# A table of priorities redrawn: the static order of a Restormer block on five engines

## The chip, the cores and the metric

The kernel runs on one core of a Trainium2 chip. The metric is the device time of one execution in microseconds (us); lower is better. All arithmetic is in float32.

## What is computed

The input x has 16 images of 128 channels and 96 x 96 pixels. One block is applied to it: a layer norm over channels, an attention whose matrix is channels by channels (8 heads of 16 channels) and which needs a sum over all pixels of an image, a residual, a second layer norm, and a feed-forward part (128 to 512 channels, a depthwise 3 x 3 convolution, a gelu, 512 back to 128 channels) with a residual.

```python
x_hwc = x.transpose(0, 2, 3, 1)
xn1 = _layernorm(x_hwc, ln1_w, ln1_b)
x = x + _attention(xn1, wq, wk, wv, wp).transpose(0, 3, 1, 2)   # softmax(l2norm(q) l2norm(k)^T) v, per head
xn2 = _layernorm(x.transpose(0, 2, 3, 1), ln2_w, ln2_b).transpose(0, 3, 1, 2)
h1 = jnp.einsum('bchw,oc->bohw', xn2, w_in[:, :, 0, 0])
h2 = lax.conv_general_dilated(h1, w_dw, ..., feature_group_count=HID)
x = x + jnp.einsum('bchw,oc->bohw', gelu(h2), w_out[:, :, 0, 0])
```

## The kernel before

**Tiling.** Channels lie on the 128 partitions. An image is cut into 8 bands of 12 rows (1152 pixels), a band into 3 units of 4 rows (384 pixels). With 16 images there are 128 bands. The 512 hidden channels are 4 chunks of 128. A job is one chunk of one band in the depthwise convolution (conv_job, L1143); in some bands the fourth chunk is done by PE instead (by_matmuls, L1259). There are 467 jobs that use the vector engines.

**Work by engine.** These are the kinds of operations, under the names that the table uses:

- PE (TensorE): forth_a, forth_b (transposes for the statistics, L868), gram (L916), back_a, back_b (transposes back, L964), mix (the attention's matrix on x, L818), hidden (128 to 512 channels, L1162), conv (nine taps by matmuls, L1274 and L1280), out (512 to 128, L1315).
- DVE (VectorE): stats_a, stats_b (L876), place_b (normalized x into the ring, L968), residual (L824), tap (multiply and add one shifted tap: L1190 for the first and the last of a job, L1194 between them), add (the last residual, L1322).
- ACT (ScalarE): copied_a, copied_b (L905, L973), place_a (L970), mixed (L827), halo (L1158), kept (the hidden chunk out of a PSUM bank, L1167), products (one tap times its weight, L1178), gelu (L1211), conv_gelu (L1292).
- POOL (GpSimd): variance_a, variance_b (L881), power_a, power_b (L885), scaled_a (L909), merge (adds a product and the unshifted chunk into the one buffer merged, L1181; a second addition at L1184), and it issues the adding transfers add_x (L830), add_last (L1203) and add_first (L1206).
- SP (SyncE) issues load_a (L795) and store (L1326).

The letters a and b stand for the first and second normalization.

**What sets the order.** The program is written out in a fixed order of instructions for every engine. Before that, a planner in the kernel (class Plan, L228) simulates the engines with a duration for each operation. An operation is ready when what it depends on is done and its buffers are free. Of the ready operations of an engine, the one with the lowest place goes first (order, L274; dispatch, L313). The resulting order is then emitted (the last lines of tile_restormer_block), and on the chip every engine takes its own instructions strictly in that order and waits for semaphores.

A place counts in jobs: an operation of job 100 has a base near 100. To it comes a number by kind, and a shift by kind and stretch, where a stretch is 15 places:

```python
def place_at(kind, place, i=1):
    of = kind if i else kind + "_0"
    return Place(place + (AT[of] + SHIFTS.get(max(0, int(place // STRETCH)), {}).get(of, 0)), RANK.get(kind, 0))
```

AT (L51) has a number for each kind, from some -3600 to some +4600. Against these, the 467 places of the whole run are few, so the sum of AT and shift mostly says which kind goes first within a stretch, and the place itself decides among operations of one kind. SHIFTS (L66) has 32 rows, one for each stretch of 15 places, and up to 53 entries in a row. Place (L219) adds RANK to the priority alone, and leaves it out of the turn in which buffers of some pools are given (IN_TURN, L50).

**Shared things.** The kinds compete for four PSUM banks (h), one accumulator of three banks (acc), the one buffer merged, 8 product buffers (pr), 8 gelu buffers (h3), 4 transposed buffers (zT), 5 and 2 bands of x (xb, x1).

Of the kernel before, what the change touches and what calls it, by code (L numbers as in the profile page):

```python
# [66 lines left out]
    0: dict(load_w=1.9, zeros=-8.4, load_a=-22.8, forth_a=-1.1, stats_a=-0.3, variance_a=-0.3, power_a=-8.1,  # L67
        merge=-300.7, gram=0.2, back_a=-0.2, place_a=-1660.1, attention=-276.4, mix=-21.7, residual=-23.2,
        mixed=530.5, forth_b=40.5, stats_b=-118.7, variance_b=14.1, power_b=605.1, back_b=0.1, place_b=1.6,
        halo=4.3, kept=986.6, products=-7.1, add_last=329.8, tap=-1.6, add_first=1.7, gelu=7.1, conv=-6,  # L70
        conv_gelu=0.4, out=0.2, add=-660.9, store=1.7, mix_0=-899, residual_0=-622, gram_0=0.9, forth_a_0=18.5,
        stats_a_0=-2.4, stats_b_0=19.6, scaled_a_0=-65.5, copied_a=-60.9, back_a_0=-6.5, back_b_0=0.2,
        place_a_0=399.7, place_b_0=1296.2, late=10.6, load_a_0=4.4, load_dw=229.6, units=8.6, variance_a_0=619.5,
        power_a_0=-469.8, variance_b_0=-341, power_b_0=-17.1),
    1: dict(load_a=-14.5, forth_a=0.1, stats_a=14.8, variance_a=1354, power_a=1176.9, merge=637, scaled_a=46.3,
        gram=-0.1, back_a=0.1, place_a=1.6, attention=-12.1, mix=-4.5, mixed=403.6, add_x=1946.3, forth_b=-6.6,
        stats_b=-1.9, variance_b=-52.3, power_b=5.8, back_b=170.3, place_b=-0.2, halo=-1066.6, hidden=-3.3,
        kept=923, products=1, add_last=-6.7, tap=0.7, add_first=1488, gelu=1.5, conv=0.7, conv_gelu=0.9, out=-0.4,
        add=2.8, copied_a=379.4),
    2: dict(forth_a=0.2, stats_a=-3.5, variance_a=-8.2, merge=0.8, scaled_a=-9.6, gram=3281.1, place_a=1229.9,  # L80
        mixed=38.9, forth_b=-125.8, stats_b=576.6, variance_b=-252.3, power_b=-0.5, back_b=-1367.9, place_b=-21.3,
        halo=-1033.7, kept=0.2, add_last=1838.5, add_first=19.2, gelu=-95.7, conv=-0.2, conv_gelu=0.1, add=-688.1,
        store=-2.9, copied_b=-10.5),
    3: dict(load_a=0.3, stats_a=-421.1, variance_a=1.7, power_a=1940.7, merge=360.1, scaled_a=19.9, gram=-3.7,
        back_a=-1.6, place_a=-1386.7, mix=-3.2, mixed=-1368.8, add_x=331.4, forth_b=9.5, stats_b=-631.1,
        power_b=84.1, place_b=-406.8, halo=-5.4, kept=976.7, products=0.3, add_last=0.8, tap=0.1, add_first=1358.3,
        gelu=2.1, conv=-2.9, conv_gelu=-0.3, add=-1929.6, store=-1489.9, copied_a=4.3),
    4: dict(load_a=-0.5, forth_a=0.4, stats_a=-0.7, power_a=24.6, merge=-2.2, scaled_a=1377.6, back_a=-152.2,
        place_a=-15.7, mixed=-9.8, add_x=2.6, forth_b=73.3, stats_b=12.2, variance_b=-15.1, power_b=-8.5,
        back_b=0.1, place_b=2076.2, halo=5, kept=185.5, products=-0.1, add_last=6.5, tap=0.5, add_first=-10.8,  # L90
        gelu=-13.4, conv=-3.1, conv_gelu=0.7, out=0.1, add=-664.4, store=1113.3, copied_a=-1138.6),
    5: dict(load_a=0.1, stats_a=-1.1, variance_a=-313.3, power_a=1.2, merge=-12.5, scaled_a=1035.8, gram=-3.2,
        back_a=-3.1, place_a=-265.5, attention=-0.6, mix=2.8, mixed=137.1, add_x=-6.9, forth_b=-29.6,
        stats_b=-638.6, variance_b=771.6, power_b=45, back_b=-404.6, place_b=146, halo=-0.5, kept=200.1,
        add_last=2.7, add_first=-1.7, gelu=-2, conv=0.4, conv_gelu=0.3, add=2.9, store=1134, copied_a=1.4,
        copied_b=18.3),
    6: dict(forth_a=-0.2, stats_a=15.7, variance_a=-46.9, power_a=976.2, scaled_a=-8.2, gram=2277.6, back_a=-2,
        place_a=-7.5, mix=0.1, mixed=-346.5, add_x=-1.2, forth_b=3.4, stats_b=0.2, variance_b=0.1, power_b=37.6,
        back_b=-0.5, place_b=1358.9, halo=49.9, kept=-465.7, products=-0.1, gelu=21, conv=-22.3, conv_gelu=0.1,
        add=-599.3, store=3342.4, copied_a=-381.6),  # L100
    7: dict(forth_a=0.2, stats_a=-1.6, variance_a=1309.9, power_a=2424.9, merge=0.2, scaled_a=4976.2, gram=-27.8,
        back_a=11.1, place_a=176.5, attention=-0.4, mix=0.7, mixed=-5.3, add_x=358.3, forth_b=7.9, stats_b=1.4,
        variance_b=-1.7, power_b=8.5, back_b=0.6, place_b=19.7, halo=1.9, kept=864.1, products=-1, add_last=342.7,
        tap=-0.6, add_first=15.3, gelu=5, conv=3346, conv_gelu=-0.5, store=1090.3, copied_a=-967.2,
        copied_b=1704.6),
    8: dict(load_a=-2.4, forth_a=1.3, stats_a=0.3, variance_a=-4.2, power_a=-4.3, merge=7.7, scaled_a=670.4,
        gram=2291.6, place_a=24.6, mix=-0.3, mixed=1600.2, add_x=-36.8, forth_b=57.3, stats_b=1042.9,
        variance_b=-17, power_b=-0.3, back_b=-0.2, place_b=2469.7, halo=-2888.4, kept=1099.2, add_last=-33.7,
        tap=0.8, gelu=-6.8, conv=-6.2, conv_gelu=0.9, out=0.1, add=-406.4, copied_a=2.7),
    9: dict(load_a=-1.9, stats_a=-0.2, variance_a=-0.1, power_a=23.8, merge=-25, scaled_a=11.3, gram=-7.9,  # L110
        back_a=-0.3, place_a=-511.8, attention=-1.8, mix=-2.4, mixed=-1119.9, add_x=320.8, forth_b=-16.7,
        stats_b=-566.6, variance_b=8.9, power_b=10.1, back_b=-0.2, place_b=-0.8, kept=-0.8, products=-0.3,
        add_last=-16.7, tap=0.3, add_first=6.8, gelu=19.2, conv=-5.3, conv_gelu=0.1, add=0.7, store=-980.3,
        copied_a=25.1),
# [5 lines left out]
    11: dict(forth_a=-0.7, stats_a=13.2, variance_a=367, power_a=5322.9, merge=-21.3, scaled_a=1837.4, gram=3416.9,  # L120
        back_a=-339.2, attention=-1, mix=-1.1, mixed=640.8, add_x=2.6, forth_b=4.6, stats_b=10.1, variance_b=-16.9,
        power_b=4.6, back_b=-0.2, place_b=565.6, halo=13.3, hidden=-0.7, kept=859.2, add_last=23.5, tap=0.7,
        add_first=-6.9, conv=1.5, conv_gelu=-0.2, add=1024.5, store=4493.9),
    12: dict(load_a=10.3, forth_a=5.5, stats_a=9.9, variance_a=-0.8, merge=-188.3, gram=0.1, place_a=-1371.9,
        mix=-1.2, mixed=-1155.8, add_x=-847.4, forth_b=-21.3, stats_b=581.5, variance_b=21.3, power_b=-52.5,
        place_b=1.1, halo=-3.3, kept=17.6, products=0.4, tap=1, add_first=9.7, gelu=14.3, conv=-0.1, out=-0.4,
        add=959.9, store=-103.4, copied_a=-1417.6),
    13: dict(load_a=-1, forth_a=-1.5, stats_a=0.3, variance_a=157, power_a=-144.7, merge=1628.9, scaled_a=23.4,
        gram=14.4, back_a=10.4, place_a=973.7, attention=-0.4, mix=-3.2, mixed=-508.1, add_x=16.4, forth_b=3.7,
        stats_b=-1506.7, variance_b=1583.4, power_b=1787.5, place_b=-0.3, halo=-2.1, kept=1321.3, products=0.7,  # L130
        add_last=-985.5, add_first=57.2, gelu=-1.1, conv=-0.4, conv_gelu=0.2, add=12.2, store=4, copied_a=0.3,
        copied_b=42),
    14: dict(load_a=9.9, forth_a=-0.7, stats_a=1.9, variance_a=920.6, power_a=-677.5, merge=14.3, gram=-1.7,
        place_a=-1663.1, mix=1.4, mixed=-558.3, add_x=52.8, forth_b=-30.6, stats_b=-645, variance_b=7.6,
        power_b=-18.6, back_b=-448.9, place_b=637.9, halo=35.3, products=-0.1, add_last=25.3, tap=-0.2,
        add_first=2.1, gelu=-10.5, conv=-0.7, conv_gelu=0.9, add=8.7, copied_a=375),
    15: dict(load_a=-1.6, variance_a=-6.2, power_a=708.9, merge=-556.4, scaled_a=2876.1, gram=0.5, back_a=68.5,
        place_a=-266, attention=-1, mix=1.8, mixed=-3.4, forth_b=11.3, variance_b=553.6, power_b=11.4, back_b=-0.7,
        halo=16.8, kept=870.2, add_last=6.4, gelu=-15.6, conv=-1.7, add=4.5, store=-113.3, copied_a=1.1,
        copied_b=-10.1),  # L140
# [12 lines left out]
        copied_b=4622.1),  # L153
# [1246 lines left out]
```

## Time and profile before

| what | value |
|---|---|
| median of 3 runs | 3971.78 us (3965.01 to 3973.48) |
| the profiled execution | 3976.05 us |
| its span, first to last instruction | 3974.3 us |
| mean granted TensorE clock | 0.998 |
| HBM read and written | 148.85 MB and 75.50 MB |
| moved by all DMA queues | 777.42 MB |

The profiled execution is 4.27 us longer than the median of the runs, and its span leaves 1.75 us for what lies around it. Most of the moved bytes are transfers from on-chip memory to on-chip memory that add: add_last and add_first, 466 of each with 576 KB.

A line of a group reads: code line, engine, operation, output and inputs by the program's names, shape, count, then busy us and mean ns of one, then the engine's idle time before such instructions and what ended it. PEld is the loading of weights that belongs to a matmul. A float32 matmul here is two instructions of each kind, a transpose one. A line of waits reads: who waited for whom, us in total, times, longest us.

### The profile page before, as it was taken

How to read it: one execution, taken by the hardware profiler on the slowest of the kernel's cores; microseconds unless marked ns; L12 is line 12 of the kernel's file. 1: busy time of each engine (PE TensorE's matmuls, PEld its weight loads, DVE VectorE, ACT ScalarE, POOL GpSimd, SP SyncE). 2: the span in 40 equal slices, each digit the busy share in tenths (PEclk: the TensorE clock that was granted, in tenths of full speed). 3: DMA queues.
4: the chain of work that ended last, by engine and by line, in shares of the span. 5: the costliest groups of instructions: out<-in, count | busy, mean ns of one | idle time of the engine just before them, and what ended most of it. 6: DMA issues, size and time to landing. Idle time of an engine off the chain costs nothing.

```text
span 3974.3 us, 50973 instructions
## 1 busy us (share of the span) xinstructions
PE 3892.4 (98%) x16760; PEld 2521.7 (63%) x16760; DVE 3834.8 (96%) x4390; ACT 3558.1 (90%) x5186; POOL 3379.4 (85%) x3107
## 2 busy tenths in 40 slices
PE   8999999999999999999999999999999999999999
PEld 7566666666666666666666666666666666665555
DVE  7999999999999999999999999999999999999998
ACT  3989989989999999999989989999899999998886
POOL 5998988898898988988888888888888888888674
PEclk9999999999999999999999999999999999999999
DMA  3999999999999999999999999999999999999996
GB/s 100 187 191 204 200 200 198 199 202 198 210 201 209 203 198 203 200 210 201 194 202 197 207 201 194 205 197 206 189 192 206 203 207 201 203 197 183 191 189 146
DMA packets 191691, 777.42 MB, mean 196 GB/s; under 512 B 22208, under 2 KB 23616, under 8 KB 191424
## 3 DMA queue, kind: packets, MB, share of 16 engines
q0 software_dynamic: 151920, 622.33, 82.6%
q1 hardware_dynamic: 38784, 151.75, 10.2%
q8 instruction: 132, 2.16, 0.2%
q14 instruction: 135, 1.11, 0.1%
q10 hardware_dynamic: 720, 0.07, 0.0%
HBM read 148.85 MB, written 75.50 MB: 56 GB/s over the span
## 4 chain that ended last, share of the span: by engine, by line
PE 58%; DVE 14%; ACT 10%; DMA 7%; POOL 6%; issue 5%; POOLq 0%; DVEq 0%; ACTq 0%
PE h L1315 15%; PE h L1162 14%; PE h L1274 13%; DVE acc L1194 6%; DMA h<-pr 5%; ACT pr L1178 5%; PE h L818 4%; PE h L964 4%; PE g L916 3%; PE h L868 3%; DVE acc L1190 3%; DVE h L1190 2%; ACT h L1167 2%; POOL merged L1181 2%; DMA pr<-pr 2%
## 5 line engine op out<-in xcount | busy, mean ns | idle before, releaser
L1178 ACT ACTIVATE pr<-h,ratio 128x1152 f32<-128x1152 f32 x1494 | 1837.2, 1271 | 37.6 <-DMA h<-pr 12.6
L1194 DVE SCALAR_TENSOR_TENSOR acc<-h,ratio,acc 128x1152 f32<-128x1152 f32 (+1 forms) x1308 | 1810.3, 1384 | 7.7
L1181 POOL TENSOR_TENSOR merged<-pr,h 128x1152 f32<-128x1152 f32 x466 | 1238.1, 2657 | 100.5 <-DVE acc L1190 54.7
L1162 PE MATMUL h<-xn,winT 128*128 128x384 f32 (+2 forms) x2802 | 1088.0, 496 | 16.0 <-ACT h L1167 9.2
L1315 PE MATMUL h<-h,woutT 128*128 128x384 f32 x3072 | 1086.2, 488 | 1.7 <-ACT h L1167 1.1
L1274 PE MATMUL h<-xn,comp 128*128 128x380 f32 (+2 forms) x2430 | 895.0, 482 | 2.2 <-ACT h L1167 1.5
L1167 ACT COPY h<-h 128x384 f32<-128x384 f32 (+2 forms) x1401 | 652.9, 493 | 192.4 <-PE h L1162 187.5
L1315 PEld LDWEIGHTS h<-h,woutT 128*128 128x128 f32 x3072 | 565.2, 190 | 359.3 <-ACT h L1167 7.8
L1162 PEld LDWEIGHTS h<-xn,winT 128*128 128x128 f32 x2802 | 500.0, 190 | 326.6 <-issue 34.2
L1190 DVE SCALAR_TENSOR_TENSOR acc<-h,ratio,merged 128x1152 f32<-128x1152 f32 x466 | 686.6, 1473 | 20.9 <-POOL merged L1184 10.1
L1206 POOL DMA_DIRECT2D h<-pr x466 | 463.3, 994 | 241.9 <-DVE h L1190 57.5
L1190 DVE SCALAR_TENSOR_TENSOR h<-h,ratio,acc 128x1152 f32<-128x1152 f32 x467 | 655.2, 1403 | 3.4
L1211 ACT ACTIVATE h<-h,ksum 128x1152 f32<-128x1152 f32 (+2 forms) x586 | 616.0, 1081 | 46.4 <-DMA h<-pr 45.6
L1274 PEld LDWEIGHTS h<-xn,comp 128*128 128x128 f32 x2430 | 430.6, 189 | 235.2 <-issue 17.1
L1203 POOL DMA_DIRECT2D pr<-pr x466 | 478.7, 1040 | 103.1 <-ACT pr L1178 73.4
L885 POOL TENSOR_TENSOR ve_b<-ve_b,mhalf 128x4 f32<-128x4 f32 x288 | 366.0, 1277 | 7.9
L909 POOL TENSOR_TENSOR zT<-zT,ve_a 128x512 f32<-128x512 f32 x270 | 331.3, 1232 | 8.6
L885 POOL TENSOR_TENSOR ve_a<-ve_a,mhalf 128x4 f32<-128x4 f32 x288 | 318.6, 1109 | 15.3
L868 PE MATMUL h<-ident,x 128*128 128x128 f32 x2244 | 317.0, 275 | 13.7 <-ACT xn L970 4.9
L868 PEld LDWEIGHTS h<-ident,x 128*128 128x128 f32 x2244 | 263.6, 142 | 96.4 <-issue 38.6
L818 PE MATMUL h<-xn,mwT 128*128 128x384 f32 x768 | 289.1, 490 | 7.7 <-ACT h L1167 3.2
L916 PEld LDWEIGHTS g<-zT 128*128 128x128 f32 x2160 | 269.9, 191 | 40.2 <-POOL zT L909 11.0
(190 smaller groups left out, 3967.0 us busy)
## 6 DMA issues: line engine op xcount, KB each, us to landing
pr<-pr POOLq DMA_DIRECT2D x466, 576.0 KB, 7.8
h<-pr POOLq DMA_DIRECT2D x466, 576.0 KB, 7.7
x<-in_x_dram SPq DMA_DIRECT2D x128, 576.0 KB, 7.5
out_dram<-x SPq DMA_DIRECT2D x127, 576.0 KB, 4.6
x<-in_x_dram POOLq DMA_DIRECT2D x123, 576.0 KB, 9.1
out_dram<-x SPq DMA_DIRECT2D x3, 192.0 KB, 1.9
h<-in_L_conv_w_in_dram SPq DMA_DIRECT2D x1, 256.0 KB, 3.4
h<-in_L_conv_w_out_dram SPq DMA_DIRECT2D x1, 256.0 KB, 3.6
```

The lines of the kernel that those rows point to most:

```text
L868: nc.tensor.transpose(d["pT", q][:, k, :], xt[:, j * P : (j + 1) * P], ident)
L885: nc.gpsimd.tensor_tensor(rstd, rstd, mhalf, ALU.pow)
L1162: nc.tensor.matmul(rows(ph), lhsT=winT[:, n, :], rhs=window(xn, r0 + r, e - r, 1), start=True, stop=True)
L1167: nc.scalar.copy(window(h1_, r, e - r, 1), rows(d.pop(("ph", r))))
L1178: nc.scalar.activation(to, shifted(t), AF.Copy, scale=ratio[:, n, t : t + 1])
L1181: nc.gpsimd.tensor_tensor(merged, d["pr", dma_taps[0]], shifted(UNIT), ALU.add)
L1190: nc.vector.scalar_tensor_tensor(to, shifted(t), ratio[:, n, t : t + 1], also, ALU.mult, ALU.add)
L1194: nc.vector.scalar_tensor_tensor(to, shifted(t)[:, lo:hi, cut], ratio[:, n, t : t + 1], to, ALU.mult, ALU.add)
L1203: nc.gpsimd.dma_start(out=d["pr", dma_taps[1]], in_=d["pr", t], accum_op=ALU.add)
L1211: nc.scalar.activation(h3, h3, AF.Gelu, bias=ksum[:, z, n : n + 1])
L1274: nc.tensor.matmul(d["pc"][:, lo:hi, cut], lhsT=comp[:, t, :], rhs=window(xn, r0 + dy, UR, dx)[:, lo:hi, cut], start=(t == order[0]), stop ...
L1315: nc.tensor.matmul(rows(d["po"]), lhsT=woutT[:, n, :], rhs=h3s[g, n][:, s * UR : (s + 1) * UR, :], start=(k == 0), stop=(k == NCH - 1),)
```

## The change

Only the table SHIFTS is new. It was searched once more, from the former table, with three other sets of scattered durations. AT, RANK, STRETCH, the planner with its durations, and all operations stay. The former table has 882 entries, the new one 917. Over both, 21 entries are equal, 162 differ by under 1, 186 by 1 to 10, 235 by 10 to 100 and 410 by 100 or more; all 32 stretches are touched. As one example, this is the stretch of places 150 to 164:

```diff
@@ -64,141 +64,142 @@
 STRETCH = 15
 SHIFTS = {
...
-    10: dict(forth_a=-0.1, stats_a=-18.6, variance_a=213.9, power_a=-1.6, merge=-0.3, scaled_a=1679, gram=3360.3,
-        back_a=-0.8, place_a=-13.6, mix=-3.6, mixed=503.8, add_x=829.5, forth_b=1.4, stats_b=16.4,
-        variance_b=1422.9, power_b=15, back_b=0.5, place_b=1532, halo=9, hidden=1.3, kept=1393.5, products=0.1,
-        add_last=-363.1, add_first=-14.8, gelu=10.8, conv=0.2, out=67.7, store=-4.8, copied_a=-32.2,
-        copied_b=-331.3),
...
+    10: dict(load_a=2.6, stats_a=16.4, variance_a=938.2, power_a=6.6, merge=4.9, scaled_a=1424.6, gram=396.2,
+        back_a=0.4, place_a=-830.2, mixed=10.6, add_x=1945, forth_b=-22.9, stats_b=951.7, variance_b=1574.8,
+        power_b=1830.9, back_b=0.5, place_b=20.4, halo=-1030.7, hidden=1.3, kept=2468.7, products=-0.1, tap=0.2,
+        add_first=504, gelu=43.3, conv=15.5, conv_gelu=-2.1, out=160.2, add=-198.4, store=1486.8, copied_a=2,
+        copied_b=1699.2),
...
 }
```

With AT at -1398.6 for power_b, -380.8 for merge and -1160.25 for variance_b, this stretch puts merge at about -376 in place of -381, power_b at 432 in place of -1384, and variance_b at 415 in place of 263: merge goes ahead of power_b there, which it did not before.

More of the change, by code (lines that the diff above doesn't have):

```diff
@@ L66 @@
 SHIFTS = {
[L67 to L114, printed above, removed]
-    10: dict(forth_a=-0.1, stats_a=-18.6, variance_a=213.9, power_a=-1.6, merge=-0.3, scaled_a=1679, gram=3360.3,
-        back_a=-0.8, place_a=-13.6, mix=-3.6, mixed=503.8, add_x=829.5, forth_b=1.4, stats_b=16.4,
-        variance_b=1422.9, power_b=15, back_b=0.5, place_b=1532, halo=9, hidden=1.3, kept=1393.5, products=0.1,
-        add_last=-363.1, add_first=-14.8, gelu=10.8, conv=0.2, out=67.7, store=-4.8, copied_a=-32.2,
-        copied_b=-331.3),
@@ L120 @@
[L120 to L140, printed above, removed]
-    16: dict(load_a=0.3, forth_a=2.3, variance_a=4292.9, power_a=-14, scaled_a=828.6, gram=344, back_a=-1160.6,
-        place_a=1228, mix=0.9, mixed=-554.1, add_x=14.9, forth_b=-60.1, stats_b=0.4, variance_b=16.5, power_b=248,
-        place_b=-4.2, halo=-7.3, kept=-576.6, products=1.4, add_last=364, tap=-0.1, add_first=2.6, gelu=-9.2,
-        conv=14.6, add=-6.2, store=3.6, copied_a=381.7),
@@ new lines @@
+    7: dict(stats_a=16.2, variance_a=1180.1, power_a=6.4, merge=9.9, scaled_a=5945.5, gram=3376.7, back_a=-6.7,
+        mix=1.1, mixed=1625.6, add_x=1518.7, forth_b=8.3, stats_b=5.6, variance_b=-22.8, power_b=-32.6,
+        place_b=2071.5, hidden=-0.2, kept=2370.2, products=-1, add_last=12.4, tap=1.3, add_first=250.1, gelu=-0.3,
+        conv=3326.3, conv_gelu=0.6, out=-0.4, add=-651.4, store=-445.2, copied_b=-571.3),
+    8: dict(load_a=-1.6, stats_a=-11.5, variance_a=925.5, power_a=-0.4, merge=5.1, scaled_a=4.7, gram=-0.2,
+        back_a=0.8, place_a=-144.1, mix=-1.6, mixed=17.3, add_x=1536.8, forth_b=92.8, stats_b=0.6, variance_b=12.2,
+        power_b=-30.5, place_b=967, halo=-5.8, kept=1374.7, products=-0.6, add_last=8.7, tap=1.2, add_first=-30.7,
+        conv=1.3, conv_gelu=1.4, out=0.1, add=-582, store=1116.1, copied_a=-69.6),
@@ new lines @@
+    9: dict(forth_a=-1.9, stats_a=40.9, variance_a=-255.6, power_a=-674.1, merge=-796.7, scaled_a=826, gram=-1.7,
+        back_a=-381.8, place_a=-585.4, attention=-0.3, mixed=450.6, add_x=4874.1, forth_b=9.1, stats_b=-1198.3,
+        variance_b=42.4, power_b=-23.7, back_b=-0.1, place_b=846.8, halo=0.4, kept=305.3, add_last=12, tap=0.3,
+        add_first=819.3, gelu=-35.9, conv_gelu=-0.2, add=-1826.8, store=-468.7, copied_a=1.8),
+    10: dict(load_a=2.6, stats_a=16.4, variance_a=938.2, power_a=6.6, merge=4.9, scaled_a=1424.6, gram=396.2,
[3 more added lines that the diff above has]
+        copied_b=1699.2),
@@ new lines @@
+    11: dict(load_a=-0.1, forth_a=-2.9, stats_a=2887.7, variance_a=-2.3, power_a=5285.6, merge=-14.4,
+        scaled_a=1846.5, gram=-2.4, back_a=-3, place_a=-1, attention=-1.7, mix=1.9, add_x=-998.6, forth_b=-15.7,
+        variance_b=1769.9, power_b=1369.2, back_b=0.1, place_b=1514.3, halo=-7, hidden=3.5, kept=1321.6,
+        add_last=-929.4, add_first=-18.4, conv=2.4, conv_gelu=-0.9, out=2.8, add=14.1, store=1500.8),
+    12: dict(load_a=0.6, forth_a=-2.9, stats_a=1745.1, variance_a=14.4, power_a=-712.4, merge=-12.6, scaled_a=11.2,
+        gram=-0.2, back_a=-1935.1, place_a=0.3, mix=-1.2, mixed=24.1, add_x=-517.4, forth_b=35.4, stats_b=-1.3,
+        variance_b=235.3, power_b=0.2, place_b=504, halo=-13.5, kept=-0.4, products=1.7, tap=0.8, add_first=259.9,
+        conv=-0.3, conv_gelu=-0.6, out=-0.4, store=536.5, copied_a=-18.7),
@@ new lines @@
+    21: dict(load_a=0.9, forth_a=2.1, stats_a=2911.2, variance_a=1.1, power_a=947.9, merge=-1028, scaled_a=1432.9,
+        gram=22.9, back_a=0.6, place_a=-2.3, attention=-0.2, mix=-5.6, mixed=490.9, add_x=419.2, forth_b=-9.3,
+        stats_b=573.6, variance_b=2791.7, power_b=-29.9, back_b=1.6, place_b=-6.6, halo=-1088.5, hidden=-0.4,
+        kept=17.9, add_last=-1032.3, tap=0.1, add_first=1026.8, gelu=-2932.3, conv=-0.1, conv_gelu=-1.9, out=-0.1,
+        add=-2019.6, store=-451.8, copied_a=167.9),
@@ new lines @@
+    26: dict(load_a=9.2, forth_a=0.7, power_a=2012.1, back_a=-36.1, place_a=-1703.7, attention=-1.7, mixed=-1.9,
+        add_x=1568.3, stats_b=1.3, variance_b=-13.9, power_b=-21.8, place_b=2576.3, halo=22.4, hidden=0.8,
+        kept=-518.6, products=1.2, add_last=0.2, add_first=-0.4, gelu=12.4, conv=1.4, conv_gelu=2.3, out=29.9,
+        add=0.6, copied_b=-12.8),
+    27: dict(load_a=-0.6, forth_a=2.7, variance_a=1411.3, power_a=5305.3, merge=4.8, scaled_a=4.8, gram=-5.4,
+        back_a=10.5, mix=-0.4, mixed=98, add_x=2015.1, forth_b=-412, stats_b=520, variance_b=1616.2,
+        power_b=3093.7, back_b=-1877.9, place_b=0.9, halo=22.6, hidden=-0.6, kept=966.9, products=-0.2, tap=-0.1,
+        add_first=-65.1, gelu=-13.1, conv=-21.2, conv_gelu=0.8, out=-0.8, add=1, store=-10.9, copied_a=-109.4),
@@ new lines @@
+    28: dict(load_a=50.9, forth_a=846.7, stats_a=16.4, variance_a=-56.5, power_a=398.6, merge=37.1, gram=-0.1,
+        back_a=-391.4, place_a=385.1, attention=40.8, mix=3.8, mixed=307.2, add_x=2.1, forth_b=-34,
+        variance_b=-3.9, power_b=-14.3, back_b=0.5, place_b=6, halo=-3.3, products=0.8, add_last=393.9,
+        add_first=1053.9, gelu=-33, conv=-1.7, conv_gelu=0.9, out=0.9, add=-14.6, store=-60.5, copied_a=-19.4),
+    29: dict(merge=778.1, mix=0.4, forth_b=-6.7, stats_b=9.7, variance_b=1573.4, power_b=1884, place_b=1329.7,
+        halo=8.1, hidden=-1, kept=0.4, products=-0.3, add_last=51.5, tap=0.5, add_first=33.1, gelu=-3385.7,
+        conv=261.8, conv_gelu=-2, out=112.3, add=-1520.7, store=3385.7, copied_b=-874.1),
@@ L202 @@
+    30: dict(merge=480.9, mix=9, mixed=-310.1, add_x=-1.5, forth_b=43, stats_b=2.6, variance_b=801.7, power_b=40.7,
+        back_b=0.2, place_b=1315.6, halo=-4118.2, kept=9.2, products=11.9, add_last=22.1, tap=0.3, gelu=-2928.8,
+        conv_gelu=0.6, add=-590.3, store=327.9),
+    31: dict(merge=836.2, hidden=60, kept=1321.4, products=997, add_last=837.7, tap=8.9, add_first=1465.2,
+        gelu=-3.8, conv=5.2, conv_gelu=427, out=-1.7, add=-540.8),
 }
```

143 lines of the change are left out of this document (86 added, 57 removed).

## The prediction

> **What bounds the kernel now.** I read the page first (busy shares, then the chain that ended last), then the view by windows for the start, the body and the end.
>
> ```profile
> span 3974.3 us, 50973 instructions
> PE 3892.4 (98%) x16760; PEld 2521.7 (63%) x16760; DVE 3834.8 (96%) x4390; ACT 3558.1 (90%) x5186; POOL 3379.4 (85%) x3107
> PE 58%; DVE 14%; ACT 10%; DMA 7%; POOL 6%; issue 5%; POOLq 0%; DVEq 0%; ACTq 0%
> ```
> ```profile
> 0.00:200.00 200.00, 184.15 (x978) 132.50 (x979) 167.37 (x292) 129.31 (x204) 147.72 (x195) 0.97 0.62 144
> 200.00:3800.00 3600.00, 3537.58 (x15207) 2288.19 (x15205) 3514.39 (x3955) 3302.57 (x4814) 3130.10 (x2835) 1.00 0.95 200
> 3800.00:3974.00 174.00, 170.68 (x580) 101.05 (x578) 153.03 (x145) 126.21 (x169) 101.54 (x80) 1.00 0.81 165
> ```
>
> The columns of the windows are PE, PEld, DVE, ACT, POOL, granted clock, DMA share, GB/s. In the body of 3600 us PE idles 62.4 us (3600 - 3537.58) and DVE 85.6 us (3600 - 3514.39), and the DMA engines are busy 0.95 of the time. So PE is the bound, DVE is 23 us behind it, and the transfers are close. The chain agrees: 58% of it is PE, and it passes to other engines for the rest.
>
> The ends of matmuls are modelled, so I also ask how short PE's own work could be. Two runs without a gap give the pitch of wide and of narrow matmuls:
>
> ```profile
> 18.37 2.84 PE L916 MATMUL g<-h 128*128 128x129 f32 x24
> 3927.16 7.90 PE L1315 MATMUL h<-h,woutT 128*128 128x384 f32 x24
> ```
> ```profile
> L1162 PE MATMUL h<-xn,winT 128*128 128x384 f32 (+2 forms) x2802 | 1088.0, 496 | 16.0 <-ACT h L1167 9.2 <-DVE xn L968 1.6 <-ACT x L827 1.5
> L1315 PE MATMUL h<-h,woutT 128*128 128x384 f32 x3072 | 1086.2, 488 | 1.7 <-ACT h L1167 1.1 <-ACT h L1211 0.2
> L1274 PE MATMUL h<-xn,comp 128*128 128x380 f32 (+2 forms) x2430 | 895.0, 482 | 2.2 <-ACT h L1167 1.5 <-DVE x L1322 0.4 <-DVE st_b L876 0.2
> L818 PE MATMUL h<-xn,mwT 128*128 128x384 f32 x768 | 289.1, 490 | 7.7 <-ACT h L1167 3.2
> ```
>
> A run of 24 lasts 23 pitches and one last matmul: (7.90 - 0.49) / 23 = 0.322 us for the wide ones, (2.84 - 0.28) / 23 = 0.111 us for the narrow. There are 2802 + 3072 + 2430 + 768 = 9072 wide and 16760 - 9072 = 7688 others: 9072 x 0.322 + 7688 x 0.111 = 2921 + 853 = 3774 us. The rest, some 200 us or 5% of the span, is the most that any order could hope for; the visible idle time is under half of it (3974.3 - 3892.4 = 82 us), because a short stall inside a run counts as busy.
>
> **The change part by part.** No instruction is added, removed or resized: the table only adds numbers to places, and a place only decides which ready operation of an engine the planner lists first. So each engine's sum of durations stays, at 0 us, and all that can move is waiting (and DVE's and POOL's stretches where both read SBUF, below). The work's order changes, though, on all queues. I count it from the two tables: for every stretch of 15 places and every pair of kinds on one engine, AT plus shift says who goes first, and I count a pair as turned when the difference changes sign and is over 15 places on both sides. On PE 40 of 1152 pairs turn, on DVE 80 of 480, on ACT 186 of 1152, on POOL 174 of 1152, on SP (load_a against store) 8 of 32. PE's own order is nearly the old one; what is reshuffled are its feeders.
>
> Term 1, the ends. The first 200 us lose 15.9 us of PE (200 - 184.15), and the last 174 lose 3.3 us. The last run of matmuls leads straight to the last addition:
>
> ```profile
> 3960.19 10.59 PE L1315 MATMUL h<-h,woutT 128*128 128x384 f32 x32
> 3970.81 0.56 DVE L1322 TENSOR_TENSOR x<-h,x 128x384 f32<-128x384 f32 x1 [2.02 <-PE h L1315]
> ```
>
> Nothing there is left to win, and the start waits for loads and for the first normalization in either order. The bounds of the two ends together are -6 us (a third of their 19.2 us) and +6 us; I take 0, since most of their idle time is dependence.
>
> Term 2, the body. How far stretches differ under one and the same recipe is seen in its 36 windows of 100 us, of which the first and last, the two best and the two worst are:
>
> ```profile
> 200.00:300.00 100.00, 97.14 (x432) 63.42 (x430) 96.53 (x113) 89.86 (x135) 91.17 (x82) 1.00 0.91 191
> 1500.00:1600.00 100.00, 100.00 (x433) 65.70 (x432) 99.23 (x111) 89.89 (x134) 87.84 (x82) 1.00 0.96 203
> 1800.00:1900.00 100.00, 100.00 (x459) 67.00 (x458) 98.82 (x110) 95.00 (x142) 89.14 (x83) 1.00 0.97 200
> 2000.00:2100.00 100.00, 95.93 (x440) 63.52 (x439) 95.94 (x112) 90.06 (x137) 86.66 (x80) 1.00 0.95 204
> 2200.00:2300.00 100.00, 95.95 (x409) 61.66 (x407) 96.09 (x110) 89.24 (x130) 90.60 (x83) 1.00 1.02 214
> 3700.00:3800.00 100.00, 98.88 (x349) 58.80 (x348) 97.72 (x102) 86.72 (x121) 68.97 (x57) 1.00 0.94 191
> ```
>
> PE's idle time is 1.73 us in the mean of the 36 (62.4 / 36), from 0.00 to 4.07, with a spread of 1.1. Two ends: if the new table only draws each stretch again, the expected change is 0, with a spread of 1.1 x 1.41 x 6 = 9 us; if it brought every stretch to the two best, it would win the whole 62.4 us. Between them lies this: the windows worse than the mean are together 16.8 us above it (the sum over the 36), and a table searched further should above all mend the bad ones. The search knows modelled, scattered durations and not the chip's, so it will not mend all: I take two thirds of 16.8, which is 11 us. As the real slack is over twice the visible, the wins may be larger than the windows show; that goes into the range.
>
> Term 3, where the gain would come from and what is late next. POOL is the queue whose order changes in the clearest direction: merge goes ahead of variance_b in 10 stretches, of power_a in 7, of power_b in 6; add_x goes ahead of power_a in 8; add_first falls back. On DVE, tap and add go ahead of place_b in 7 and 8 stretches.
>
> ```profile
> DVE acc L1190 <- POOL merged L1184: 10.1, 15, 1.5
> POOL merged L1181 <- DVE acc L1190: 54.7, 79, 3.0
> PEld h L964 <- POOL ve_b L885: 12.7, 24, 2.1
> PEld g L916 <- POOL zT L909: 11.0, 12, 2.2
> PEld h L964 <- POOL zT L909: 6.4, 8, 1.9
> PE g L916 <- POOL zT L909: 6.5, 6, 1.6
> PE h L964 <- POOL ve_b L885: 4.1, 6, 1.9
> PE h L964 <- POOL zT L909: 4.1, 4, 1.7
> ```
> ```profile
> L1190 DVE SCALAR_TENSOR_TENSOR acc<-h,ratio,merged 128x1152 f32<-128x1152 f32 x466 | 686.6, 1473 | 20.9 <-POOL merged L1184 10.1 <-POOL merged L1181 4.2 <-DVE h L1190 0.5
> L885 POOL TENSOR_TENSOR ve_b<-ve_b,mhalf 128x4 f32<-128x4 f32 x288 | 366.0, 1277 | 7.9
> ```
>
> An earlier merge can save at most what DVE waits before the operation that reads it, 20.9 us, and DVE is not the last bound, so less reaches the end. What is late next is then what the merge went past: the variance, power and scaling operations, on whose results (ve_b, zT) PE waits: 12.7 + 11.0 + 6.4 us in weight loads and 6.5 + 4.1 + 4.1 in matmuls, 44.8 us at the most. I cost this term at 0 net, with the bounds -20.9 and, as the rival below, +21. Its cover is POOL's own idle time, 470 us in the body (3600 - 3130.10).
>
> The sum: 0 - 11 + 0 = -11 us against the profiled execution, 3976.05 us (span 3974.3 and 1.75 around it): 3965.05. The median of the three runs, 3971.78, lies 4.27 below that execution, so the forecast is 3965.05 - 4.27 = 3960.8, rounded **3961 us**.
>
> **The port.** One resource can change durations. The accumulation that reads merged has both tensors in SBUF, as POOL's merge has:
>
> ```profile
> L1181 POOL TENSOR_TENSOR merged<-pr,h x466: 2405/2635/3738, 84.7 to 3939.3; 128x1152 f32<-128x1152 f32 x156
> L1190 DVE SCALAR_TENSOR_TENSOR acc<-h,ratio,merged x466: 1396/1417/3192, 87.2 to 3942.1; 128x1152 f32<-128x1152 f32 x156
> ```
>
> Its median is 1.417 us, its mean 1.473, its worst 3.192: a few are held up, and the mean's excess over the shortest is 466 x (1.473 - 1.396) = 36 us of DVE time. The Trainium skill (SBUF — State Buffer, "Who interferes with whom") says that such a DVE instruction contends with a GpSimd instruction that reads SBUF, and that the one issued second waits. The trace agrees, by the 3.192. The rule speaks against the change only as far as moved merges meet this operation more often; that is the third rival.
>
> **The rivals.** *No difference* (0.28): the search fits the durations it was given, the stretches are drawn again, and the sum stays within 8 us: 3972 us. For it: the spread of 9 us, and that PE's order hardly changes. Against: a spread of 9 leaves only six in ten within 8.
>
> *POOL's queue holds PE* (slower, 0.20): a merge put further ahead stands at the head of POOL's queue until the accumulation before it has read the single buffer merged (54.7 us, 79 times already), and the variance and power behind it wait, then PE's transposes. There are 466 / 32 = 14.6 merges in a stretch, so 10 turned stretches hold 146; each can stand for the 1.83 us that a power (1.277) and a variance (0.55 by the row below) would have taken: 267 us of POOL.
>
> ```profile
> L881 POOL TENSOR_SCALAR ve_b<-st_b 128x4 f32<-128x4 f32 x288 | 155.5, 547 | 18.4 <-DVE st_b L876 17.9
> ```
>
> Of POOL's 595 us of idle time (3974.3 - 3379.4), those 44.8 us are about 8%, so 267 becomes 21 us at the most and, with half of each stand, 11. I price it at +14, which is 3986 us. It decides once those waits of PE together pass about 59 us (44.8 + 14).
>
> *The port* (slower, 0.05): if the held-up accumulations doubled, 36 us more of DVE, of which DVE's lead of 23 us over PE's idle absorbs most: +13, which is 3985 us. It decides once the mean of that group passes 1.52 us (1.473 + 23 / 466).
>
> *The change mends more* (in the forecast's sign): every bad stretch to the mean and the hidden stalls with them, twice 16.8, is -34: 3938 us.
>
> **How the numbers follow.** The forecast, a gain of 8 us or more, has 0.47; no difference 0.28; slower 0.25 (0.20 + 0.05). A difference under 0.2%, 8 us, can't be told from no change here. The range reaches from 3940 (the whole gain of 34, less the little that lies beyond) to 3991 (the slower rivals, with 5 us of the ends). The likeliest case alone spans 3940 to 3964.
>
> **What would show it.** Right: instruction counts and the busy sums of ACT and of DVE stay within 0.3%; PE's idle time in the body falls from 62.4 to about 50, by the worst windows (2000, 2200) coming up; DVE's idle time before the accumulation on merged falls below 20.9. The queue rival: PE's waits on ve_b and zT pass 44.8 clearly. The port rival: the mean of 1.473 rises. Wrong would be a body whose good windows (1500, 1800) got worse by as much as the bad ones got better, or one whose waits moved to ACT's copies out of the banks: kept falls back there in more stretches than it goes ahead, and PE already waits 9.2 us on it at L1162.

## The result and the profile after

The kernel with the new table takes 3976.82 us (median of 20 runs), the one before 3971.86 us (median of 20 beside it). The ratio is 1.0019, with a 95% interval of 1.0012 to 1.0026: the new table is slower by 5 to 10 us. That is about the bound of 0.2% at which this measurement tells anything, and the interval leaves out 1. The time lies inside the range of the prediction and on the wrong side of its forecast.

The profiled executions can't show that loss: the new table's took 3974.48 us, 1.6 us less than the one before, whose 3976.05 us is longer than any of its 20 times here (3963.4 to 3974.1). The 20 times of the new table fall into two groups, eleven from 3973.7 to 3977.5 us and nine from 3980.3 to 3985.5, and all its profiles (three executions) are of the lower group. What the profiles do show well is the course of the work, and the study rests on that.

The page and the three stretches of the kernel after. Its code lines are one higher (L1190 is now L1191).

```profile
span 3972.8 us, 51018 instructions
PE 3888.8 (98%) x16760; PEld 2519.3 (63%) x16760; DVE 3829.3 (96%) x4390; ACT 3557.3 (90%) x5186; POOL 3386.7 (85%) x3107
PE 60%; DVE 13%; POOL 9%; ACT 9%; issue 5%; DMA 3%; POOLq 0%; DVEq 0%; ACTq 0%
```
```profile
0.00:200.00 200.00, 181.23 (x975) 130.71 (x976) 167.10 (x291) 128.65 (x203) 147.46 (x194) 0.99 0.62 144
200.00:3800.00 3600.00, 3538.39 (x15212) 2288.14 (x15211) 3512.29 (x3960) 3305.89 (x4820) 3143.24 (x2838) 1.00 0.96 200
3800.00:3974.00 174.00, 169.20 (x576) 100.47 (x574) 149.87 (x142) 122.81 (x165) 96.02 (x76) 1.00 0.79 162
```

Counts and sums stayed, as they had to: the same 16760, 4390, 5186 and 3107 instructions, DVE within 0.2% and ACT within 0.1%. PE's idle time in the body is 61.6 us (3600 - 3538.39), against 62.4 before and about 50 in the forecast.

Four of the 100 us windows, the two that were best and the two that were worst before:

```profile
1500.00:1600.00 100.00, 99.77 (x431) 64.65 (x430) 98.89 (x114) 91.12 (x135) 92.11 (x89) 1.00 0.97 202
1800.00:1900.00 100.00, 97.78 (x441) 64.18 (x440) 97.01 (x109) 91.11 (x138) 93.11 (x84) 1.00 0.95 197
2000.00:2100.00 100.00, 98.63 (x441) 65.11 (x440) 97.14 (x112) 92.40 (x141) 85.57 (x79) 1.00 0.97 209
2200.00:2300.00 100.00, 98.94 (x416) 63.13 (x415) 97.65 (x110) 92.20 (x133) 85.99 (x81) 1.00 1.02 212
```

The worst came up by 2.7 and 3.0 us and the best fell by 0.2 and 2.2. Over all 36 windows the sum stayed, with a spread of 1.0 us against 1.1 before, and the windows worse than the mean are together 15.3 us above it, against 16.8: the idle time moved to other places. The prediction had named good windows that get worse as a sign of being wrong.

PE's waits on POOL's results, the point at which the queue rival was to be recognised, in the kernel after:

```profile
PEld h L965 <- POOL ve_b L886: 18.8, 27, 2.1
PEld g L917 <- POOL zT L910: 8.0, 9, 2.9
PEld h L965 <- POOL zT L910: 7.8, 10, 2.1
PE h L965 <- POOL ve_b L886: 9.1, 14, 1.4
PE h L965 <- POOL zT L910: 4.8, 4, 1.5
PE g L917 <- POOL zT L910: 4.5, 4, 2.7
```

They sum to 53.0 us, 8.2 more than the 44.8 before, and stay under the 59 from which that rival was to decide. And the operation that reads merged, in the view of that buffer:

```profile
L1182 POOL TENSOR_TENSOR merged<-pr,h x466: 2410/2626/4143, 85.4 to 3937.1; 128x1152 f32<-128x1152 f32 x156
L1191 DVE SCALAR_TENSOR_TENSOR acc<-h,ratio,merged x466: 1397/1416/3720, 87.9 to 3940.4; 128x1152 f32<-128x1152 f32 x156
```

Its shortest and its median are as before. Its mean went from 1.473 to 1.467 us (683.6 us of busy time in place of 686.6), so the port rival did not happen.

Two more signs that the prediction had named are on the page after:

```profile
L1163 PE MATMUL h<-xn,winT 128*128 128x384 f32 (+2 forms) x2802 | 1080.7, 495 | 15.5 <-ACT h L1168 4.2
L1191 DVE SCALAR_TENSOR_TENSOR acc<-h,ratio,merged 128x1152 f32<-128x1152 f32 x466 | 683.6, 1467 | 23.3 <-POOL merged L1185 13.1
```

DVE's idle time before the operation that reads merged rose from 20.9 to 23.3 us, where the forecast had it fall. PE's wait on ACT's copies before the hidden matmuls fell from 9.2 to 4.2 us, so the waits did not move to those copies.

### The profile page after: what moved, and what is told of

The parts are those of the page before. It is cut to its first block, busy times and chain, and to the rows that moved or that the text cites. A ratio compares the mean times of both kernels' runs of the same rounds, so it can differ in the third digit from the quotient of the medians.

```text
span 3972.8 us, 51018 instructions
## 1 busy us (share of the span) xinstructions
PE 3888.8 (98%) x16760; PEld 2519.3 (63%) x16760; DVE 3829.3 (96%) x4390; ACT 3557.3 (90%) x5186; POOL 3386.7 (85%) x3107
## 4 chain that ended last, share of the span: by engine, by line
PE 60%; DVE 13%; POOL 9%; ACT 9%; issue 5%; DMA 3%; POOLq 0%; DVEq 0%; ACTq 0%
PE h L1316 16%; PE h L1163 14%; PE h L1275 13%; DVE acc L1195 6%; ACT pr L1179 4%; PE h L965 4%; PE h L819 4%; PE g L917 4%; PE h L869 3%; DVE acc L1191 2%; POOL merged L1182 2%; DMA h<-pr 2%; DVE h L1191 2%; ACT h L1168 2%; POOL zT L910 1%
## 5 line engine op out<-in xcount | busy, mean ns | idle before, releaser
L1182 POOL TENSOR_TENSOR merged<-pr,h 128x1152 f32<-128x1152 f32 x466 | 1251.4, 2685 | 100.9 <-DVE acc L1191 48.9
L1191 DVE SCALAR_TENSOR_TENSOR acc<-h,ratio,merged 128x1152 f32<-128x1152 f32 x466 | 683.6, 1467 | 23.3 <-POOL merged L1185 13.1
L1207 POOL DMA_DIRECT2D h<-pr x466 | 474.5, 1021 | 237.2 <-DVE h L1191 64.3
L1212 ACT ACTIVATE h<-h,ksum 128x1152 f32<-128x1152 f32 (+1 forms) x586 | 618.9, 1088 | 52.8 <-DMA h<-pr 48.4
L1191 DVE SCALAR_TENSOR_TENSOR h<-h,ratio,acc 128x1152 f32<-128x1152 f32 x467 | 654.7, 1402 | 3.9 <-PE h L1316 0.3
L886 POOL TENSOR_TENSOR ve_b<-ve_b,mhalf 128x4 f32<-128x4 f32 x288 | 375.0, 1308 | 9.2
L910 POOL TENSOR_TENSOR zT<-zT,ve_a 128x512 f32<-128x512 f32 x270 | 342.0, 1272 | 7.2
L886 POOL TENSOR_TENSOR ve_a<-ve_a,mhalf 128x4 f32<-128x4 f32 x288 | 334.3, 1165 | 13.7
```

The source lines that it names most:

```text
L886: nc.gpsimd.tensor_tensor(rstd, rstd, mhalf, ALU.pow)
L1182: nc.gpsimd.tensor_tensor(merged, d["pr", dma_taps[0]], shifted(UNIT), ALU.add)
L1191: nc.vector.scalar_tensor_tensor(to, shifted(t), ratio[:, n, t : t + 1], also, ALU.mult, ALU.add)
L1212: nc.scalar.activation(h3, h3, AF.Gelu, bias=ksum[:, z, n : n + 1])
```

## The theory that came out of the result, and its rivals

Two numbers had not been asked for ahead of the prediction: how long the two orders are by the planner's own durations. Played through in the emitted order, each engine strictly in turn and each operation with the duration that the planner gives it, the table before ends at 3914.2 us and the new one at 3927.1 us, 12.9 us later. All numbers below that are called the plan are this one, for each table. They are the kernel's model and no measurement; whether the chip follows them is the question.

**Plan theory**: the chip carries out the order as planned, each order loses some 50 us against its plan (it ends that much later than planned), and differences between plans come back as differences of time. Its rivals are the **redraw theory** (each stretch is an independent draw of idle time, on which the forecast and its range stood) and the **POOL theory** (the queue rival of the prediction).

The course speaks for the first only in part. Of the 384 last additions (L1322, L1323 after), the start of every 48th in the two profiles, new minus before, in us:

```
addition              48     96    144    192    240    288    336    384
chip, new - before   -0.1   -2.4    3.4    1.5   -2.7   -1.2    2.7   -1.6
plan, new - before   -0.8   -1.1    4.4    5.6    6.6    7.8   12.0   12.9
```

At the first three of these marks the chip repeats the plan's ups and downs within 1.3 us; with two later executions of the new table (repeat and again_b, below) it is within 2.8 and 3.5 us, so these small differences alone don't decide. After that the new table's execution gains on its plan, relative to the other, by some 14 us in this pair of profiles. Three executions of the new table agree with one another within 2.8 us at every one of the 384 additions, and rows29_31 (below), whose order is that of the table before up to some 3600 us, agrees with it within 3.7 us up to there, so the gain is more than the noise of one profile. A few us of it can be the clock: its mean is 0.999 in the profile after and 0.998 in the one before.

## The experiments

The kernels differ in the table alone; the planner then makes another order from it. Each is compared with the table before on the same chip.

**The new table again** (repeat).

```diff
 SHIFTS = {
-    0: dict(load_w=1.9, zeros=-8.4, load_a=-22.8, ...   # all 32 rows
+    0: ...                                              # all 32 rows of the new table
```

> The new table again, nothing else changed. If the two groups of times seen for it (nine or ten near 3974.5 us and as many near 3980 to 3985 us) belong to the program, both come again here, and none of the table before beside it goes over 3975. If the +5 of the median was chance between runs, the median falls within 2 us of the table before.

Measured: 3976.24 us against 3970.97, ratio 1.0018 (1.0009 to 1.0027), times from 3972.6 to 3976.2 (six) and 3979.4 to 3983.6 (five). The loss is real, and so are the two groups, though less far apart. But the times beside it reached 3976.03, over the 3975 that was expected.

A third execution of the same kernel was recorded for its course (again_b).

> The new table once more, for a second profile of the same program. Its times so far fall in two groups, near 3974.5 and near 3982 us; the two profiles so far are of the lower group (3974.48 and 3976.24). If this execution is of the upper group, its course against the earlier profile shows whether the 8 us come in one place (one transfer or one stall that falls the other way) or spread evenly over the run. If it is of the lower group, it shows how far two profiles of one order differ along the run: under 3 us is expected.

Measured: 3974.52 us, in the lower group once more, and the course quoted above held: within 2.8 us of the other two at all 384 additions. What sets the upper group therefore wasn't seen.

**Rows 29 to 31, and rows 16 to 23, from the new table** (rows29_31, rows16_23).

```diff
-    16: dict(...), ... 23: dict(...)      # rows of the table before
+    16: dict(...), ... 23: dict(...)      # the same rows of the new table; all others as before
```

> The table before, with rows 29 to 31 (the last 60 us of places and what follows) from the new one. Plan theory (the chip carries out the order as the planner in the kernel laid it out, so differences of the planner's end come back on the chip): the planner ends this order 10 us later than the table before, all of it in the last two images of the run, so +10 us (+7 to +13) and no difference before 3600 us. Redraw theory (each stretch is a new draw of its idle time): three stretches of 32, so 0 with a spread of 3 us. POOL theory (the queue of POOL holds PE): 0 to +2 us.

> The table before, with rows 16 to 23 from the new one. Plan theory: the planner ends this order 53 us later, with nothing before 2060 us and most of it between 2500 and 3200 us: +53 us (+38 to +60). Redraw theory: eight stretches, 0 with a spread of 5 us, between -10 and +10. POOL theory: a quarter of the turned pairs, +1 to +4 us.

Measured: rows 29 to 31 gave 3974.63 us, ratio 1.0011 (1.0002 to 1.0020), +4 where the plan says +10: below the plan's +7 to +13 and above the POOL theory's +2, and it settles nothing. Rows 16 to 23 gave 4027.4 us, ratio 1.0145 (1.0131 to 1.0159), +56 where the plan says +53. A quarter of the rows costs ten times as much as the whole change, and far more than the 10 us that the redraw theory allowed: idle time isn't drawn stretch by stretch.

**POOL's kinds alone from the new table, and all kinds but POOL's** (pool_new, pool_old).

```diff
-    10: dict(..., variance_a=213.9, power_a=-1.6, merge=-0.3, scaled_a=1679, ...)
+    10: dict(..., variance_a=938.2, power_a=6.6, merge=4.9, scaled_a=1424.6, ...)   # and so in all rows
```

> The table before, with only POOL's kinds (variance, power, scaled, merge and the adding transfers) from the new one in all 32 rows. POOL theory: this carries the whole loss, +5 to +21 us, and PE's waits on POOL's results pass 59 us. Redraw theory: 0 with a spread of 9 us. Plan theory: the planner ends this order 150 us later, spread over the whole run, so +150 us (+110 to +160), with the waits spread over all engines and not on POOL's results alone.

> The new table with POOL's kinds put back to the numbers of before in all rows: the change without its POOL part. POOL theory: back to the time before, 3972 us within 8. Plan theory: the planner ends this order 219 us later than the table before, so 3971 + 219 = 4190 us and up to 40 more.

Measured: POOL's part alone 4149.54 us, ratio 1.0451 (1.0437 to 1.0466), +179 with a plan of +150, which is over the +160 that was expected at the most; the change without POOL's part 4202.3 us in a single execution, +232 with a plan of +219. The POOL theory falls in both directions: neither half of the change is the change's cost, and the halves alone cost 36 and 46 times the 5 us of both together. In pool_new's profile the waits of PE on POOL's results rise, but not as the whole of it:

```profile
PEld h L964 <- POOL ve_b L885: 34.5, 33, 3.8
PEld g L916 <- POOL zT L909: 22.3, 25, 2.2
PE h L964 <- POOL ve_b L885: 22.0, 17, 3.6
PE g L916 <- POOL zT L909: 11.5, 17, 1.6
```

These are 90 us, where the same four were 34 before. All waits of PE and of its weight loads on other engines, which partly overlap, rise by some 280 us: 130 on ACT's results, 86 on DVE's, 50 on POOL's and 13 on transfers.

**One number changed** (merge_12).

```diff
-    12: dict(load_a=10.3, forth_a=5.5, stats_a=9.9, variance_a=-0.8, merge=-188.3, gram=0.1, ...
+    12: dict(load_a=10.3, forth_a=5.5, stats_a=9.9, variance_a=-0.8, merge=211.7, gram=0.1, ...
```

> The table before with one number changed: merge in row 12 from -188.3 to 211.7, so that POOL's merges go further behind in places 180 to 194. Plan theory: the planner ends this order 94 us later; up to 1500 us it is the same program, then it loses some 3 us in every later stretch, as the rows behind were tuned to a course that no longer comes: +94 us (+70 to +115). POOL theory (merges ahead hold PE): a gain of up to 1 us in that stretch, and nothing after it. A local theory (a stretch's idle time depends on its own row alone): between -3 and +6 us.

Measured: 4063.29 us, ratio 1.0236 (1.0221 to 1.0252), +93 where the plan says +94. The views by windows, the table before first and merge_12 second, tell where it goes:

```profile
200.00:1400.00 1200.00, 1181.12 (x5133) 767.28 (x5131) 1172.83 (x1325) 1103.25 (x1617) 1054.71 (x963) 1.00 0.96 201
1600.00:2000.00 400.00, 394.77 (x1712) 257.08 (x1711) 393.39 (x442) 372.09 (x541) 351.37 (x318) 1.00 0.96 202
2000.00:2800.00 800.00, 783.03 (x3397) 508.74 (x3396) 778.40 (x880) 731.10 (x1069) 698.39 (x635) 1.00 0.95 200
2800.00:3600.00 800.00, 784.01 (x3394) 508.88 (x3393) 778.18 (x881) 734.66 (x1069) 700.72 (x638) 1.00 0.95 200
```
```profile
200.00:1400.00 1200.00, 1185.01 (x5152) 771.50 (x5151) 1174.79 (x1330) 1105.51 (x1621) 1057.96 (x964) 1.00 0.96 202
1600.00:2000.00 400.00, 382.19 (x1637) 245.41 (x1637) 381.21 (x429) 361.24 (x525) 342.55 (x310) 1.00 0.93 193
2000.00:2800.00 800.00, 770.54 (x3274) 494.56 (x3273) 751.85 (x846) 705.06 (x1029) 677.43 (x607) 0.99 0.93 194
2800.00:3600.00 800.00, 762.52 (x3249) 483.55 (x3247) 746.54 (x839) 694.51 (x1019) 666.18 (x607) 1.00 0.91 190
```

Up to 1400 us the two are nearly alike. From 1600 to 3600 us every stretch does less: DVE's busy time is 26 us lower in 2000 to 2800 and 32 us lower in 2800 to 3600, some 3 to 4% of it, although row 12 covers only 15 of the 467 places, near 1500 us. The additions tell the same: merge_12 starts the 144th 5 us before the table before, and the 192nd, 240th, 288th and 336th 14, 31, 60 and 88 us after it; from there to the last the distance stays. The rows behind are unchanged, and they were good only for the course that used to come to them.

**Fresh tables from other searches** (fresh_short, fresh_long, fresh_scatter). They start from the table before and change row after row from the front, keeping for each row what brings the work of the next two rows forward most.

```diff
-    0: dict(...), ... 31: dict(...)      # the table before
+    0: dict(...), ... 31: dict(...)      # other numbers, some 900 entries as before
```

> A third table, from a short search of another kind (row after row from the front, 400 trials in a row, only the planner's own durations, none scattered). The planner ends its order 5.6 us later than the table before and 7.3 us earlier than the new one. Plan theory: +6 us on the table before (0 to +13), within a few us of the new table. If the scattered durations of the new table's search made it lose less between plan and chip, this table lacks that, and lands above the new one, at +6 to +15. Redraw theory has fallen already; it would say 0 with a spread of 9.

> A table from the same search as fresh_short with six times the trials (2400 in a row), again on the planner's own durations alone. The planner ends its order at 3896.7 us, 17.5 us earlier than that of the table before (3914.2). Plan theory without more: 3970 - 17.5 = 3953 us. With the loss between plan and chip that fresh_short had (70 us, where the table before has 57 and the new one 50): 3967 us, so -4 on the table before. If a search on the planner's own durations only picks courses that the chip cannot keep, 3975 us or more.

> A table from the same search as fresh_short (500 trials in a row), but every trial judged by the planner's course played with its own durations and with three sets scattered by 10%. The planner ends its order at 3912.4 us, 1.8 us earlier than that of the table before. Plan theory without more: 3968 us. If scattered durations in the search are what lowers the loss between plan and chip, it is near 50 us as for the new table: 3962 us. If the loss has nothing to do with them, it can be as for fresh_short, 70 us: 3982 us.

Measured: fresh_short 3990.0 us, ratio 1.0052 (1.0039 to 1.0064); fresh_long 3972.97 us, ratio 1.0006 (0.9997 to 1.0015), which can't be told from no change; fresh_scatter 3985.49 us, ratio 1.0040 (1.0027 to 1.0053). Here the plan theory alone misses by 14 to 20 us. These three lose 70, 76 and 73 us against their plans (3919.8, 3896.7 and 3912.4), where the table before loses 56 to 58 and the new one 50. A plan that is 17.5 us shorter bought nothing. Scattered durations of my kind in the search (each operation by itself, 10%) did not lower that loss.

**Only the rear half searched again** (rear_again).

```diff
     0: dict(...), ... 12: dict(...)      # kept
-    13: dict(...), ... 31: dict(...)
+    13: dict(...), ... 31: dict(...)      # searched afresh
```

> The table before with only rows 13 to 31 searched again, row after row from the front as for fresh_scatter (1600 trials in a row, own and scattered durations), so that the first half keeps its order and its course. The planner ends this order at 3907.0 us, 7.2 us earlier than that of the table before, all of it after 2300 us. Plan theory: -7 us (-10 to -3), 3963 us. In the second half all tables so far lost about alike against their plan (29 to 33 us for the three fresh ones, 31 for the table before, 22 for the new), so no larger loss is expected. If any table searched afresh loses 13 us more than its plan says, as the three fresh ones did over the whole run, +6 us at the most.

Measured: 3959.86 us against 3969.73, ratio 0.9976 (0.9966 to 0.9986): 10 us faster than the table before, where the plan says 7, and the fastest kernel of this study. Its windows, below those of the table before:

```profile
200.00:2300.00 2100.00, 2065.49 (x8967) 1341.84 (x8964) 2053.34 (x2323) 1931.58 (x2826) 1844.24 (x1678) 1.00 0.96 202
2300.00:3800.00 1500.00, 1472.09 (x6242) 946.35 (x6241) 1461.05 (x1633) 1370.98 (x1989) 1285.86 (x1158) 1.00 0.95 198
```
```profile
200.00:2300.00 2100.00, 2068.16 (x8982) 1344.70 (x8981) 2053.87 (x2325) 1934.52 (x2831) 1848.06 (x1680) 1.00 0.96 202
2300.00:3800.00 1500.00, 1482.69 (x6287) 952.14 (x6286) 1467.31 (x1645) 1381.20 (x2004) 1298.97 (x1167) 1.00 0.96 199
```

Up to 2300 us, where its plan is the old one's, PE's work differs by 2.7 us; in the 1500 us after that PE does 10.6 us more and POOL 13 us more in the same time. The gain is where the plan has it. In the whole body PE idles 49.1 us (3600 - 3550.86), where it was 62.4 before. Whether the kept front or the larger number of trials than for fresh_scatter (1600 in place of 500 in a row) made this table hold to its plan is not separated.

All together, in us against the table before on the same chip (0.2% is 8; pool_old is a single execution):

```
kernel          plan    chip     chip's time less its plan
new table      +12.9    +5.0     50
rows29_31      +10.1    +3.7     50
rows16_23      +52.6   +56.4     61
merge_12       +93.9   +93.2     55
pool_new      +150.1  +178.6     85
pool_old      +219.4  +232       69
fresh_short     +5.6   +19.9     70
fresh_scatter   -1.8   +15.3     73
fresh_long     -17.5    +2.8     76
rear_again      -7.2    -9.9     53
before           0       0       56 to 58
```

## Why the prediction was wrong

**What bounds the kernel** held. PE is the bound, DVE and the transfers are close behind, and sums of work did not move.

**Term 1, the ends, at 0**: right within its bounds. The first 200 us lose 18.8 us (before 15.9), the last 174 lose 4.8 (before 3.3), though part of the latter is that this execution ended 1.5 us earlier.

**Term 2, the body, at -11**: this is the step that failed. In place of falling by 11 us, PE's idle time in the body went from 62.4 to 61.6 us. The term took the 36 windows as draws under one recipe, and supposed that "a table searched further should above all mend the bad ones". In its place the runs show that a window's idle time belongs to a course of the whole program: one changed number in row 12 costs 93 us, 3 to 4% of DVE's work from 2000 to 3600 us, and a quarter of the new rows costs 56. So a bad window can't be lifted by its own row alone. What the new table offers is another complete course, with its bad windows at other places and, in these profiles, about the same idle time. A search can lessen it, as rear_again shows with 49.1 us; that the search for this table would was a supposition, and the two thirds of 16.8 us had no measurement behind them.

Why the new table ends 5 us later (7.5 by the ratio) and not at the same time stays open. By the planner's own durations its course is 12.9 us longer, which has the right sign; but the three fresh tables miss their plans by 14 to 20 us, so a plan doesn't settle a difference of this size. The spread of 9 us that served for a redraw looked right only because both tables are finished courses: the finished ones measured here lie at -10 to +20 us, mixtures of two tables at +4 to +232.

**Term 3, POOL's order, at 0 net**: the number was fair and its reason was not. Counting turned pairs by kind says little. PE's waits on POOL rose by 8.2 us, as the queue rival had it, and DVE's idle time before the operation on merged rose from 20.9 to 23.3 us, where an earlier merge was to lower it. Yet PE's idle time as a whole hardly moved (84 us in the profile after, 82 before). And 40 turned pairs on PE did not mean that PE's order hardly changes: of the 6262 operations that the planner lists for PE, 5064 stand at another place of its order than before. A pair of kinds that is not turned still leaves open when each operation becomes ready, and that is up to the feeders.

**The port**: right that it would not matter, but the reason took the wrong pair. None of the 466 operations that read merged runs beside a merge, in the profile before or after: the next merge waits until the one buffer has been read. All 45 of them that took over 1.5 us before, the one of 3.192 us among them, ran beside the scaling on POOL (L909). So moved merges could not meet this operation more often; moved scalings could have.

**The forecast's sign**: wrong, and its 0.47 with it. Both "no difference" at 3972 and the queue rival at 3986 were nearer than 3961. By its size, 5 us, the change is a case of the first, but the reason given there, stretches drawn again one by one, fell with rows16_23; and PE's waits on POOL stayed below the 59 us from which the queue was to decide.

What is left open. Why a search with scattered durations gave a longer plan can't be read from these runs; that the new table loses 6 to 8 us less against its plan than the one before is measured, but that the scattered durations are the cause is not shown (fresh_scatter speaks against it, for the scatter tried there). Why the new table's times fall into two groups is open as well: no profile of the upper group was taken. It is not the mean granted clock, which in the first 20 times is 0.997 to 1.000 in the upper group and 0.997 to 0.999 in the lower.

## What to carry to other kernels

A static order made by a list planner is one course, and its parts don't add up: don't cost a changed priority by the stretch it stands in, and don't look for the guilty part by mixing two tables. Compare the planned ends of the two whole orders first; here differences of 50 us and more came back on the chip to within 20%, and differences of 5 to 20 us drown in what each course loses against its plan. When such a table is to be improved, keep the front, whose course is known to hold on the chip, and search the rear again: one table here gained 10 us in this way.

## What the runs showed of the hardware

**The clock can fall after 3.4 us in which PE was idle for 2 us.** Windows of the table before, around 2434 us, and of merge_12, around 2189 us:

```profile
2430.40:2433.86 3.46, 1.47 (x5) 0.36 (x3) 3.35 (x6) 3.34 (x8) 3.37 (x3) 1.00 1.05 208
2433.86:2437.27 3.41, 3.41 (x12) 2.70 (x13) 2.99 (x3) 2.44 (x5) 2.15 (x3) 0.50 1.05 205
```
```profile
2185.50:2189.00 3.50, 1.53 (x9) 0.99 (x9) 3.50 (x6) 3.50 (x6) 3.50 (x6) 1.00 0.67 126
2189.01:2192.40 3.39, 3.39 (x15) 2.78 (x12) 3.39 (x4) 3.39 (x6) 3.39 (x4) 0.50 1.01 176
2192.40:2195.80 3.40, 3.40 (x9) 2.15 (x9) 3.29 (x6) 0.05 (x1) 2.19 (x3) 0.50 1.07 214
2195.80:2199.20 3.40, 3.40 (x7) 1.78 (x6) 2.86 (x3) 2.33 (x3) 1.32 (x2) 0.50 1.04 198
```

In the first, PE is busy for 1.47 of 3.46 us, idle in two gaps of 0.65 and 1.34 us, and the next 3.41 us run at half the clock. In merge_12, after 1.53 of 3.50 us with gaps of 0.37 and 1.60 us, the half clock lasted 10.2 us, though PE was busy throughout. The Trainium skill (TensorE: Matmul & The Clock Gate, "Why this matters for your kernels") asks for no idle gap of PE over some 3 us; in these two traces shorter gaps, 2 us together, were enough. They did not always have this effect: in fresh_long PE was busy for 1.50 of the 3.41 us from 1297.80 us on, and the next 3.42 us still ran at the full clock.

So part of what an order loses beyond its plan can be the clock. By the mean granted clock, 0.989 in pool_new's profile and 0.998 in that of the table before, it is about 46 us (4150 x 0.011) and 8 us (3974 x 0.002) of full-speed time, and the difference of 38 us is of the size of the 28 us by which pool_new exceeded its plan's difference. That the one is the cause of the other is not shown. For the fresh tables it is not the clock: fresh_scatter loses 73 us against its plan with a mean of 0.999 in its profile. The profile of rear_again has a mean of 1.000.

**The chip repeats an order closely.** Three profiled executions of the new table never differed by more than 2.8 us at any of the 384 additions, over 3970 us and 51,000 instructions, and the instructions of each engine came in the same order in all three.
